# Moving operand copies, a row of maxima, a division and a projection by a few steps in an adaLN transformer block

## The chip, the core and the metric

The kernel runs on one core of one Trainium2 chip. The time is the device time of one execution in microseconds (us); of several runs the median is given. The core's engines work beside each other, each through its own instructions in order: TensorE (PE, matrix multiplication), VectorE (DVE), ScalarE (ACT), GpSimd (POOL), and SyncE (SP), which here issues nearly all DMA transfers. They wait for each other through semaphores.

## The reference

A transformer block on x of shape (4, 1024, 256), fp32, with conditioning vectors c that give shifts, scales and gates (sa, ca, ga, sb, cb, gb) per batch:

```python
h = _layernorm(x) * (1 + ca) + sa
x = x + ga * attention(h)            # 16 heads of 16 columns, softmax over 1024 keys
h = _layernorm(x) * (1 + cb) + sb
x = x + gb * ffn(h)
```

The attention is the usual one: `softmax(q k^T / 4) v`, then a projection. The second part, per 256 rows of x in the reference's shapes, is applied here per batch: 8 pairs of an encoder and a decoder reconstruct h (`relu(h W_enc + b) W_dec + b`); the one with the least mean squared error is chosen, and the chosen one's low-rank adapter (`relu(h W_down + b) W_up + b`) is added to a base product `h W_base + b`.

## The kernel before

**Tiles and steps.** Each batch has 16 heads, taken in 4 groups of 4 (`groups`, one entry per batch b and group g). Queries are split into two halves of 512, keys into 8 tiles of 128. One step handles one key tile for one group and one half of the queries, so a group takes `STEPS` = 16 steps and the whole run 256. In each step PE forms the transposed scores `pt` (L707; twice, for two pairs of heads), ACT takes their exponential into `es` (L715), and PE multiplies that with V into `pv` (L664, `weigh`), which also gathers the sum of exponentials. `pt` is a sum of two products: k times q, and a second matmul that subtracts the row maxima, held in the tile `mt` (two of them, for even and odd groups). A step cannot finish `pt` before its `mt` is there.

**Row maxima.** They are computed a group ahead, by `row_max` (L557): 32 pairs of scores `ps` for each group (L604), each reduced by DVE (L611), 16 pairs for each half of the queries. `wanted` (L1175) says how many pairs are to be done by a given step: a straight line between three points, the first one 19 pairs at step 0, the second 32 at step `NT - LEAD` = 3, the last 512 at step 243. When a half is complete, `to_row` (L562) turns the maxima into a row: PE transposes them (`pmx`, L564), DVE copies the result (`mfull`, L566), POOL splits it in two (`mrow`, L569 and L570), SP stores it to DRAM (`mdram`, L573) and brings it over into `mt` (L584). `defer(n, f)` calls f n steps later; outside the opening (`alone`), `store` comes one step after `to_row`, and `back` one step after that. They only fix places in SP's order: what SP waits for are semaphores.

**Operands.** Per batch and half of the columns, `qk_chunk` computes q and k in two parts and stores them to DRAM (L417, 1 MB each). `fetches` (L1185) brings the operands of each later group back by `expand` (L514): 8 copies of 256 KB on SP for each group (L525), due `n * STEPS + 1` for the n-th entry of `groups[2:]`, and only once the q and k they need are stored.

**Who decides the order.** PE's and SP's instructions are emitted in the order written out by the loop at L1281. It runs over pairs of steps and follows a pattern of letters: t for half a step's `pt`, S for scores of the row maxima, V for a step's `pv`, D for a tile of dense work, R for a decoder. Items of dense work lie in streams with conditions (`need`, `wait`, `at`); `to_row` is an item in the stream `urgent`, taken after the first V of a pair of steps. After step 16 the order on ACT, DVE and POOL is set by a scheduler.

**The end of a batch** (`post`, L721): projection of the attention result (`project`, L752), normalisation, encoders and decoders (L793, L814 to L822), `choose` (L833) with its gathers from DRAM, the two halves of `narrow` (L901: `pmid`, the chosen adapter's first product), and `final` (L958). It is spread over the next batch's steps. For the last batch part of it runs in the last steps and the rest after the loop (L1334 to L1348), where `all_of` takes a fixed number of items from one set of streams after another.

**Division.** The attention result is divided by its sums. In the last group the sums come straight from `ou` into `last_su`, and `scaled_last` (L646) does the reciprocal and the product on DVE, in two pieces of 256 columns: for the first half of the queries two steps after step 240, for the second after the loop.

Of the kernel before, what the change touches and what calls it, by code (L numbers as in the profile page):

```python
# [26 lines left out]
def tile_adaln_block(  # L27
# [22 lines left out]
    B, S, D = x.shape  # L50
    NE, _, FH = w_enc.shape
    R = w_down.shape[2]
    NT = S // P
    NC = D // P
    NG = D // (HG * HD)
    GC = P // (HG * HD)
    NPAIR = NE // 2
    SCALE = HD ** -0.5
    HALF = 512
# [220 lines left out]
    FULL = 0.86  # L280
# [4 lines left out]
    def defer(steps, f):  # L285
        later.append([steps, f])
# [8 lines left out]
    spare, alone, over = [0], [True], []  # L295
# [261 lines left out]
    def row_max(b, g):  # L557

        n = (b * NG + g) % 2
        mx = st.tile([P, NH, NH, HG, TH], F32, tag="mx", name=f"mx_{b}_{g}", bufs=2)  # L560

        def to_row(hq):  # L562
            pm = msc_tile([P, P], f"pmx_{b}_{g}_{hq}")
            nc.tensor.transpose(pm, mpad[n], ident)  # L564
            mfull = st.tile([HG * NT, P], F32, tag="mfull", name=f"mfull_{b}_{g}", bufs=1)
            nc.vector.tensor_copy(mfull, pm[: HG * NT, :])  # L566
            mrow = st.tile([HG * NT, 2, P], F32R, tag="mrow", name=f"mrow_{b}_{g}", bufs=1)
            eng = nc.vector if alone else nc.gpsimd
            eng.tensor_copy(mrow[:, 0, :], mfull)  # L569
            eng.tensor_tensor(mrow[:, 1, :], mfull, mrow[:, 0, :].bitcast(F32), ALU.subtract)  # L570

            def store():
                nc.sync.dma_start(  # L573
                    mdram[n][hq].rearrange("l r c -> r l c"),
                    mrow[hq * HG * TH : (hq + 1) * HG * TH].bitcast(F32),
                )
                if alone:
                    back()
                else:
                    defer(1, back)  # L580

            def back():
                for a in range(2):
                    nc.sync.dma_start(  # L584
                        mt[n][a * DUO : a * DUO + HG, hq * HALF : (hq + 1) * HALF].bitcast(F32),
                        mdram[n][hq, :, a * HG * TH // 2 : (a + 1) * HG * TH // 2, :].rearrange(
                            "l (i t) c -> l i (t c)", i=HG // 2
                        ),
                    )

            if alone:
                store()
            else:
                defer(1, store)

        for half in range(NH):
            pairs = [(i, half, t, h) for h in range(NH) for i in range(2) for t in range(TH)]
            for i, hq, t, h in pairs:
                q, k = duos["q", b, g, i], duos["k", b, g, i]
                t0 = hq * HALF + t * P  # L600
                ps = big_tile([P, 2, HALF], f"ps_{b}_{g}_{hq}_{t}_{h}_{i}")
                for a in range(2):
                    r = slice(a * DUO, (a + 1) * DUO)
                    nc.tensor.matmul(  # L604
                        ps[:, a, :],
                        q[r, t0 : t0 + P],
                        k[r, h * HALF : (h + 1) * HALF],
                        start=True,
                        stop=True,
                    )  # L610
                nc.vector.tensor_reduce(mx[:, h, hq, i::2, t], ps, AX.X, ALU.max, negate=True)  # L611
                if (i, hq, t, h) == pairs[-1]:
                    rows = mpad[n][:, : HG * NT].rearrange("p (q j t) -> p q j t", q=NH, t=TH)
                    nc.vector.tensor_tensor(rows[:, half], mx[:, 0, half], mx[:, 1, half], ALU.min)
                    defer(1, lambda half=half: urgent.append(("D", 0.0, [lambda: to_row(half)])))
                yield
# [26 lines left out]

    last_su = {}

    def scaled_last(h):  # L646
        su, part = last_su[h], aT_of[B - 1, h][:, NC - 1, :]
        for u in range(2):
            cols = slice(u * HALF // 2, (u + 1) * HALF // 2)
            nc.vector.reciprocal(su[:, cols], su[:, cols])  # L650
            nc.vector.tensor_tensor(part[:, cols], part[:, cols], su[:, cols], ALU.mult)

    def step_of(b, g):

        n = b * NG + g
        va = vaug[n % NV]
        ch, r0 = g // GC, (g % GC) * HG * HD
        acc = {}

        def weigh(h, kt, es):  # L660
            if kt == 0:
                acc[h] = accp.tile([P, HALF], F32, tag="acc", name=f"pv_{b}_{g}_{h}")
            for j in range(HG):
                nc.tensor.matmul(  # L664
                    acc[h][j * STRIP : (j + 1) * STRIP, :],
                    va[:, kt, j, :],
                    es[j // 2][:, j % 2, :],
                    start=(kt == 0),
                    stop=(kt == NT - 1),
                )  # L670
            if kt == NT - 1:
                if (b, h) not in aT_of:
                    aT_of[b, h] = wp.tile([P, NC, HALF], F32, tag="aT", name=f"aT_{b}_{h}", bufs=3)
                ou = wp.tile([P, HALF], F32, tag="ou", name=f"ou_{b}_{g}_{h}", bufs=1)
                nc.scalar.copy(ou, acc[h])
                to = slice(r0, r0 + HG * HD)
                at = aT_of[b, h][to, ch, :]
                if (b, ch) == (B - 1, NC - 1):
                    nc.sync.dma_start(at, ou[0::2, :])
                if (b, ch) == (B - 1, NC - 1):  # L680
                    if h not in last_su:
                        last_su[h] = wp.tile([P, HALF], F32, tag="su", name=f"su_{b}_{ch}_{h}", bufs=1)
                    nc.sync.dma_start(last_su[h][to, :], ou[1::2, :])
                    if g == NG - 1 and h < NH - 1:
                        defer(2, lambda: scaled_last(h))
                        defer(4, lambda: done.add((b, ch, h)))
                    return
                j0 = (g % GC) * HG

                def keep():  # L690
                    nc.sync.dma_start(at, ou[0::2, :])
                    nc.sync.dma_start(sdram[ch * NH + h][j0 : j0 + HG, :], ou[1::STRIP, :])
                    if g % GC == GC - 1:
                        defer(1, lambda: turned(b, ch, h))
                        defer(8, lambda: done.add((b, ch, h)))

                defer(1, keep)

        def begin(h, kt, i, es):

            pt = big_tile([P, 2, HALF], f"pt_{b}_{g}_{h}_{kt}_{i}")
            hs = slice(h * HALF, (h + 1) * HALF)
            q, k = duos["q", b, g, i], duos["k", b, g, i]
            for first in (True, False):
                for a in range(2):
                    r = slice(a * DUO, (a + 1) * DUO)
                    nc.tensor.matmul(  # L707
                        pt[:, a, :],
                        k[r, kt * P : (kt + 1) * P] if first else picks[i][r, :],
                        q[r, hs] if first else mt[n % 2][r, hs],  # L710
                        start=first,
                        stop=not first,
                    )
            e = wp.tile([P, 2, HALF], F32, tag="es", name=f"es_{b}_{g}_{h}_{kt}_{i}", bufs=4)
            nc.scalar.activation(e, pt, AF.Exp, scale=SCALE)  # L715
            es.append(e)

        return begin, weigh


    def post(b, last=False):  # L721
# [256 lines left out]
        recs.append(("done", (b, "r")))  # L978
        tail = [("need", (b, "r")), ("wait", 3), ("D", 0.1, [choose]), ("X", gate_out)]
        tail += [("X", lambda u=u: biased(u, "gbb")) for u in range(NT // 2)]  # L980
        tail += [("wait", 1), ("D", FULL, [lambda c=c: narrow(c) for c in range(NC)]), ("wait", 1)]
        each = [(u, t) for u in range(NT // 2) for t in range(2)]
        if last:
            first = [v for v in each if early(v[0])]
# [11 lines left out]
    STEPS = NH * NT  # L996
# [177 lines left out]

    def wanted(k):  # L1175

        ends = [(0, FIRST + 3), (NT - LEAD, PAIRS), (len(order) * NT - NT - LEAD, len(groups) * PAIRS)]
        for (k0, n0), (k1, n1) in zip(ends, ends[1:]):
            if k < k1:
                return n0 + (n1 - n0) * (k + 1 - k0) // (k1 - k0)  # L1180
        return ends[-1][1]
# [3 lines left out]
    def fetches():  # L1185

        moves = []
        for n, (b, g) in enumerate(groups[2:]):
            moves += [("at", n * STEPS + 1)] + [("need", (w, b, g // GC)) for w in "qk"]
            moves += [("X", lambda b=b, g=g, i=i: expand(b, g, i)) for i in range(2)]  # L1190
            if n + 2 >= NV:
                moves += [("need", ("v", b, NT // 2 - 1)), ("X", lambda b=b, g=g: fetch_v(b, g))]
        return moves
# [202 lines left out]
```

## Time and profile before

| what | us |
|---|---|
| median of 3 runs (lowest, highest) | 1140.43 (1139.66, 1143.99) |
| profiled execution, device time | 1141.97 |
| profiled execution, span of the program | 1140.1 |
| PE busy | 1079.2 |
| DVE busy | 797.2 |
| ACT busy | 702.6 |
| loop's last `pt` ends | 1070.4 |

The span is the time from the first to the last instruction of the program in the profiled execution. A group's row in the profile names the line, the engine, the operation, what it writes and reads, and the mean duration; in the timeline a bracket at the end of a row gives the idle time of that engine before it and what ended it. A wait is put down to the one that came last.

### The profile page before, as it was taken

The numbers are of one execution on the slowest core, as the hardware profiler recorded it, in microseconds if no ns is written. First come the engines' busy times: TensorE is split into PE (matmuls) and PEld (weight loads), VectorE is DVE, ScalarE is ACT, GpSimd is POOL, SyncE is SP. The second block draws the span as 40 slices with busy tenths as digits, with TensorE's granted clock in tenths as the row PEclk, the third lists the DMA queues.
The fourth block names the chain that finished last, engine by engine and source line by source line (L and its number), as shares of the span: only waits on it lengthen the run. The fifth ranks groups of instructions, "written<-read, shape, count | busy, mean of one in ns | idle before, by whom it ended". The sixth has DMA issues, their size and how long they took to land. (4 is left out here: it accounts for less than half of the span.)

```text
span 1140.1 us, 16544 instructions
## 1 busy us (share of the span) xinstructions
PE 1079.2 (95%) x6371; PEld 482.7 (42%) x6371; DVE 797.2 (70%) x958; ACT 702.6 (62%) x953; POOL 262.3 (23%) x309
## 2 busy tenths in 40 slices
PE   8989899999999999999999999999998999999995
PEld 3433334443444444444544443333544334334433
DVE  5687677667767676777678777877688777872373
ACT  3246566666556677776455777776465677754672
POOL 2214234213243121112435100003221000041103
PEclk9899999999999999999999999999999999999997
DMA  6522423232340302123150303021140200002001
GB/s 185 103 66 90 153 78 119 85 118 71 130 153 39 126 16 91 53 78 100 53 183 6 128 7 99 16 83 27 57 142 2 90 8 16 20 23 85 20 0 49
DMA packets 57799, 84.63 MB, mean 74 GB/s; under 512 B 24940, under 2 KB 40324, under 8 KB 55928
## 3 DMA queue, kind: packets, MB, share of 16 engines
q1 hardware_dynamic: 55824, 80.16, 21.9%
q0 software_dynamic: 1088, 2.36, 0.8%
q8 instruction: 50, 0.82, 0.3%
q10 hardware_dynamic: 808, 1.05, 0.3%
q14 instruction: 29, 0.24, 0.1%
HBM read 52.15 MB, written 24.06 MB: 67 GB/s over the span
## 5 line engine op out<-in xcount | busy, mean ns | idle before, releaser
L611 DVE TENSOR_REDUCE mx<-ps 128x2 f32<-128x1024 f32 x512 | 614.5, 1221 | 196.8 <-PE ps L604 191.2
L715 ACT ACTIVATE es<-pt 128x1024 f32<-128x1024 f32 x512 | 509.4, 1021 | 250.0 <-PE pt L707 229.4
L664 PE MATMUL pv<-es,vaug 128*32 128x512 f32 x2048 | 274.8, 607 | 0.5
L604 PE MATMUL ps<-k,q 64*128 64x512 f32 x1024 | 238.9, 458 | 15.9 <-DVE mx L611 11.6
L707 PE MATMUL pt<-q,k 64*128 64x512 f32 x1024 | 231.1, 435 | 11.1 <-DVE mx L611 7.7
L707 PE MATMUL pt<-mt,pick 64*128 64x512 f32 x1024 | 209.9, 393 | 3.7 <-DMA mt<-mdram 3.7
L604 PEld LDWEIGHTS ps<-k,q 64*128 64x128 f32 x1024 | 97.7, 184 | 223.2 <-issue 91.8
L707 PEld LDWEIGHTS pt<-q,k 64*128 64x128 f32 x1024 | 99.9, 185 | 116.0 <-DVE mx L611 87.7
L822 ACT ACTIVATE df<-df,fbias 128x512 f32<-128x512 f32 x128 | 91.1, 713 | 56.2 <-DVE df L817 56.2
L707 PEld LDWEIGHTS pt<-mt,pick 64*128 64x128 f32 x1024 | 100.6, 186 | 16.4 <-DMA mt<-mdram 4.0
L817 DVE TENSOR_TENSOR df<-pr,h2T 128x1024 f32<-128x1024 f32 x64 | 77.4, 1223 | 21.4 <-PE pr L814 14.9
L664 PEld LDWEIGHTS pv<-es,vaug 128*32 128x32 f32 x2048 | 40.6, 108 | 102.0 <-issue 90.4
L569 POOL CAST mrow<-mfull 32x128 fp32r<-32x128 f32 x31 | 8.7, 281 | 278.6 <-DVE mfull L566 270.7
L814 PE MATMUL pr<-he,wdec 64*128 64x512 f32 x256 | 64.6, 601 | 3.3 <-ACT es L715 3.2
L793 PE MATMUL ph<-h2T,wenc 128*128 128x512 f32 x128 | 62.4, 615 | 0.5 <-ACT h2T L350 0.4
L928 PE MATMUL pf<-wbg,h2T 128*128 128x256 f32 x128 | 37.6, 426 | 1.9 <-DVE x L948 1.9
L319 POOL TENSOR_TENSOR rstd_n<-ve_n,neghalf 128x4 f32<-128x4 f32 x16 | 16.5, 1031 | 86.3 <-DVE ve_n L317 83.5
L505 POOL COPY vaug<-vi 128x512 f32<-128x512 f32 x13 | 8.5, 657 | 111.1 <-DMA vi<-vdram 85.7
L793 PEld LDWEIGHTS ph<-h2T,wenc 128*128 128x128 f32 x128 | 22.0, 189 | 28.4 <-issue 25.2
L466 PE MATMUL pvp<-wqkv,hT 128*128 128x256 f32 x128 | 33.0, 404 | 0.0
L814 PEld LDWEIGHTS pr<-he,wdec 64*128 64x128 f32 x256 | 23.1, 185 | 22.3 <-ACT es L715 6.3
L801 ACT ACTIVATE he<-ph,fbias 128x512 f32<-128x512 f32 x32 | 22.0, 686 | 16.7 <-PE ph L793 16.7
(150 smaller groups left out, 786.0 us busy)
## 6 DMA issues: line engine op xcount, KB each, us to landing
q<-qdram SPq DMA_DIRECT2D x56, 256.0 KB
k<-kdram SPq DMA_DIRECT2D x56, 256.0 KB
qdram<-qhl SPq DMA_DIRECT2D x7, 1024.0 KB
kdram<-khl SPq DMA_DIRECT2D x7, 1024.0 KB
xin<-in_L_attn_x_dram SPq DMA_DIRECT2D x16, 256.0 KB
vdram<-vo SPq DMA_DIRECT2D x16, 256.0 KB
aT<-ou SPq DMA_DIRECT2D x32, 128.0 KB
x<-in_L_attn_x_dram SPq DMA_DIRECT2D x8, 512.0 KB
```

Source lines behind the costliest of these rows:

```text
L466: nc.tensor.matmul(pv[:, t, :], hT[:, c, t0 : t0 + P], wqkv[:, c, 2 * D : 3 * D], start=(c == 0), stop=(c == NC - 1),)
L604: nc.tensor.matmul(ps[:, a, :], q[r, t0 : t0 + P], k[r, h * HALF : (h + 1) * HALF], start=True, stop=True,)
L611: nc.vector.tensor_reduce(mx[:, h, hq, i::2, t], ps, AX.X, ALU.max, negate=True)
L664: nc.tensor.matmul(acc[h][j * STRIP : (j + 1) * STRIP, :], va[:, kt, j, :], es[j // 2][:, j % 2, :], start=(kt == 0), stop=(kt == NT - 1),)
L707: nc.tensor.matmul(pt[:, a, :], k[r, kt * P : (kt + 1) * P] if first else picks[i][r, :], q[r, hs] if first else mt[n % 2][r, hs], start=f ...
L715: nc.scalar.activation(e, pt, AF.Exp, scale=SCALE)
L793: nc.tensor.matmul(s["ph"], wenc[:, c, 2 * pr : 2 * pr + 2, :].rearrange("p n h -> p (n h)"), s["h2T"][:, c, hs], start=(c == 0), stop=(c ...
L801: nc.scalar.activation(s["he", pr, h], s["ph"], AF.Relu, bias=benc_of(pr))
L814: nc.tensor.matmul(two[:, i, :], wdec[r, pr, c * P : (c + 1) * P], he[r, :], start=True, stop=True)
L817: nc.vector.tensor_tensor(df, two, h2T[:, c, hs].unsqueeze(1).to_broadcast([P, 2, HALF]), ALU.subtract)
L822: nc.scalar.activation(df[:, i, :], df[:, i, :], AF.Square, bias=bdec_of(e, c), accum_out=s["acc"][:, e, c, h : h + 1],)
L928: nc.tensor.matmul(po[u][:, t, :], s["h2T"][:, c, t0 : t0 + P], s["wbg"][:, c, :], start=(c == 0), stop=False,)
```

## The change

There are five edits. In `row_max`, the row of the second half of group 0 (`soon`) is stored and brought over at the place where it is made, without the two deferrals; all other rows are as before, the first half's included. In `scaled_last`, the division of the last group is done in four pieces of 128 columns; for the first half of the queries the pieces stand in steps 242, 243, 244 and 245, and the half counts as done at step 246, not 244. For batches 0 to 2, `narrow` waits two steps after `choose` and the additions, not one. In `wanted`, the second point lies at step 5, not 3, so that the line that follows starts two steps later and ends where it did. In `fetches`, the operands of the first later group (n = 0) are due at step 15, not 1; for all others `max` gives the old step.

```diff
+        soon = b + g == 0
...
-                if alone:
+                if soon:
                     back()
                 else:
                     defer(1, back)
...
-            if alone:
+            if soon:
                 store()
             else:
                 defer(1, store)
...
-    def scaled_last(h):
+    def scaled_last(h, us=range(4)):
         su, part = last_su[h], aT_of[B - 1, h][:, NC - 1, :]
-        for u in range(2):
-            cols = slice(u * HALF // 2, (u + 1) * HALF // 2)
+        for u in us:
+            cols = slice(u * HALF // 4, (u + 1) * HALF // 4)
             nc.vector.reciprocal(su[:, cols], su[:, cols])
             nc.vector.tensor_tensor(part[:, cols], part[:, cols], su[:, cols], ALU.mult)
...
-                        defer(2, lambda: scaled_last(h))
-                        defer(4, lambda: done.add((b, ch, h)))
+                        for u in range(4):
+                            defer(2 + u, lambda u=u: scaled_last(h, [u]))
+                        defer(6, lambda: done.add((b, ch, h)))
...
-        tail += [("wait", 1), ("D", FULL, [lambda c=c: narrow(c) for c in range(NC)]), ("wait", 1)]
+        tail += [("wait", 1 if last else 2), ("D", FULL, [lambda c=c: narrow(c) for c in range(NC)]), ("wait", 1)]
...
-        ends = [(0, FIRST + 3), (NT - LEAD, PAIRS), (len(order) * NT - NT - LEAD, len(groups) * PAIRS)]
+        ends = [(0, FIRST + 3), (NT - LEAD + 2, PAIRS), (len(order) * NT - NT - LEAD, len(groups) * PAIRS)]
...
-            moves += [("at", n * STEPS + 1)] + [("need", (w, b, g // GC)) for w in "qk"]
+            moves += [("at", max(n * STEPS + 1, STEPS - 1))] + [("need", (w, b, g // GC)) for w in "qk"]
```

## The prediction

> **What bounds the kernel now.** I read the page's busy rows first, then what TensorE (PE) waits for, then the timeline around each place that the diff names.
>
> ```profile
> PE 1079.2 (95%) x6371; PEld 482.7 (42%) x6371; DVE 797.2 (70%) x958; ACT 702.6 (62%) x953; POOL 262.3 (23%) x309
> PEclk9899999999999999999999999999999999999997
> ```
>
> PE is busy 95% of 1140.1 us, and executes in order, so what is to be gained or lost is its idle time: 54 us over the span. About 4 us of it lies in the first steps (57 to 85 us, waits for VectorE, DVE), 8.9 in the tail after the loop (from 1073), the rest is scattered. The view of PE's waits has these among its rows:
>
> ```profile
> PE ps L604 <- DVE mx L611: 11.6, 26, 1.5
> PE pt L707 <- DVE mx L611: 7.7, 11, 1.2
> PE pt L707 <- DMA mt<-mdram: 3.7, 1, 3.7
> PE pf L928 <- DVE x L948: 1.9, 1, 1.9
> ```
>
> Total, number, longest. Two single stalls stand out. The first (3.66 us, step 16) is the row of maxima `mt` landing late; the second (1.91 us at 1028 us) is PE waiting for DVE while `scaled_last(0)` divides. The timeline of step 16 names the culprit:
>
> ```profile
> 118.84 0.32 SPq L573 DMA_DIRECT2D mdram<-mrow  x1
> 119.26 1.16 SPq L525 DMA_DIRECT2D q<-qdram  x2
> 120.47 1.22 SPq L525 DMA_DIRECT2D k<-kdram  x2
> 121.74 1.23 SPq L525 DMA_DIRECT2D q<-qdram  x2
> 123.01 1.24 SPq L525 DMA_DIRECT2D k<-kdram  x2
> 124.30 1.31 SPq L584 DMA_DIRECT2D mt<-mdram  x2
> 128.59 0.97 PE L707 MATMUL pt<-mt,pick 64*128 64x512 f32 x2 [3.66 <-DMA mt<-mdram]
> ```
>
> Eight operand copies (L525) stand in SP's queue between the row's store (L573) and its way back (L584). All other 31 rows come in time, most with 5 to 10 us to spare.
>
> **The chain that the change leans on.** An undisturbed row, from PE's transpose to the way back:
>
> ```profile
> 145.49 0.33 PE L564 MATMUL pmx<-ident,mpad 128*128 128x128 f32 x1
> 145.92 0.28 DVE L566 COPY mfull<-pmx 32x128 f32<-32x128 f32 x1 [0.65 <-PE pmx L564]
> 146.27 0.28 POOL L569 CAST mrow<-mfull 32x128 fp32r<-32x128 f32 x1 [23.84 <-DVE mfull L566]
> 146.63 0.45 POOL L570 TENSOR_TENSOR mrow<-mfull,mrow 32x128 fp32r<-32x128 f32 x1
> 147.11 0.33 SPq L573 DMA_DIRECT2D mdram<-mrow  x1
> 148.56 1.38 SPq L584 DMA_DIRECT2D mt<-mdram  x2
> ```
>
> Store 1.62 us after the transpose, way back 3.07 to 4.45, its last packet 5.49 (the trace's DMA packets); at step 16 PE resumed 0.4 after the last packet. So a clean row needs **5.9 us** from `pmx` to its first use. Now its first use is about 12 us after `pmx` (145.5 to 157.6).
>
> **Part 1, the pace (`NT - LEAD + 2`).** The built order of both programs shows what a shift of 2 in one table entry does: `to_row` moves two steps later for every row from step 8 to step 120 (15 rows; from step 128 on the rounding to pairs of steps gives the old places). `pmx` then stands in the pair of steps just before its use. What PE has left between them is 3 `ps` pairs, 5 `pt` pairs, one `pv` set, and whatever tile of dense work falls there. The old trace prices this as the time from the end of the `pv` two steps later to the use: 5.2 us with a tile (152.4 to 157.6, and five more alike), 3.2 with none (242.9 to 246.2), 6.1 with a tile and a pair. The slack of two steps is spent, and the chain is longer than most of the rooms. Row by row, with what the new order puts in the way:
> - steps 8, 40, 56, 72, 88: clean, 5.9 - 5.2 = 0.7 each, 3.5 in all.
> - step 24: an `rstd` (1.03) stands between the two `mrow` operations on POOL: 1.7.
> - steps 32, 64, 80: a 1 MB store of `khl` or `qhl` now stands between the row's store and way back. The old row of step 88 had that and landed at 6.18 instead of 5.49, so 6.6 - 5.2 = 1.4; at 80 POOL is a little late as well, 1.7. Together 4.5.
> - step 48: such a store and no tile: 6.6 - 3.25 = 3.35.
> - steps 96, 104: room 6.1, nothing. Step 112: 0.5. Step 120: 0.4.
> - step 16: below.
>
> That is 13.95 us. Nothing covers it, as PE waits in order with all later work behind it.
>
> **Part 2, operands from step 15.** The copies of group 2 were issued at step 13, when their sources were ready, and now at step 15. But the row of step 16 has moved by the same two steps, and the built order of SP is the old one: store, eight copies, way back. Store at 1.6, way back 5.46 later, issue 1.31, and 2.98 to the use as at 125.61 to 128.59: 11.35 against a bare room of 3.25. The stall of 3.66 becomes **8.1**, so +4.4. The copies themselves are wanted at step 21 and are not late. The other groups' dates do not change (`max` binds for n = 0 alone).
>
> **Part 3, `soon`.** The row of step 8 is now issued without the two deferrals. SP has nothing else between, and waits on semaphores rather than steps; worth 0 here. If that cover went, it would be a step, some 4 us.
>
> **What the slower start returns.** DVE had 13 reductions of 1.2 us to do in three steps, and now has five steps. Of the 4.06 us that PE idles from 57 to 85 us I take back 2.5 (bounds 0 and 4).
>
> **Part 4, division in pieces.** Two reciprocals of 256 columns take 1.75 us each; four of 128 should take about half each, plus a small overhead. At most it saves the 1.91 stall and the slow clock after it (1.7), and at least nothing, since DVE's sum of work in steps 241 to 245 is unchanged and its own reductions for `ps` are late next: I take -2.5. One rule speaks against counting on more. The multiply of L651 took 0.36 to 0.41 us three times and 1.53 once, while POOL was adding `gbb` to `x`. The Trainium skill (SBUF — State Buffer, its rules on the shared port pair) says that a DVE operation with two SBUF inputs and a GpSimd operation that reads SBUF lock each other out for the whole instruction. By the row, four pieces cost four times 0.2; by the rule, each piece may wait for a POOL addition (1.25 us), 4 us more. The additions are 5 us long in all and the pieces are now spread over four steps, so one or two meet them.
>
> **Part 5, narrowing two steps behind.** All four `pmid` (541.7, 790.8, 1014.8, 1125.2) start without idle time on PE: nothing to gain. It delays batch 2's output, hence the load of `x` for batch 3 (step 247 to 249) and the first projection (251 to 253; `done` at +6 alone would allow it). The second projection then is the last tile of the loop, and its normalisation, hidden beside steps 254 and 255 until now, is exposed: from the end of `ppj` (1067.14) to the first transpose is 4.6 us, of which 2.7 lie beside the last `pv`: 1.9. Then `ppj_3_2` comes after one `ph` instead of four, and the last division (5.3 us after `pv` for the DMA, then 2.0 for two pieces) makes it wait 2 us. The decodes begin about 10 us later but with three `he` already out, and ACT, which sets the end (14 squares, each with a read of its sum, in 9.99 us without a break), catches most of that up. I count **+2.8** (0 to 5).
>
> **The clock.** Each half-speed stretch in the clock record is 3.41 us and costs 1.7. In the loop there are three, after stalls of 3.66, 1.21 and 1.91 us; stalls of 1.53, 1.20, 1.20 and 1.16 had none. The Trainium skill (TensorE: Matmul & The Clock Gate, What's actually happening) says that the clock halves after at least one idle window of about 3.4 us. By the rule only step 16's stall would pay, as it does now: +0. By the rows, step 48's 3.35 pays 1.7, and of the four of 1.4 to 1.7 about one: I take **+3** and keep 0 and 10 as bounds.
>
> **Sum.** 13.95 + 4.4 - 2.5 - 2.5 + 2.8 + 3 = +19.2 us. Stalls also let DVE catch up, so some of the 19.3 us of `mx` waits vanish: about -1. The profiled execution took 1141.97 (span 1140.1), 1.5 above the median of 1140.43; on the median the sum gives **1158.5**.
>
> **Rivals.**
> - *Only the bare rows stall.* If the chain is nearer to 5 us than 5.9, steps 16 and 48 alone pay: 4.4 + 2.7 + 2 - 5 + 2.8 = +7, 1147. For it: the 0.7 of five rows is small beside what I can measure of a landing. Against it: every clean row in the trace agrees within 0.2.
> - *The clock falls at each stall.* Then 11 stalls cost 1.7 each: 1174. For it: 1.21 us was enough once. Against it: four like it were not.
> - *Faster.* One mechanism: the evener pace frees DVE early, and the row still arrives before step 16's use because SP gets to it ahead of the copies. Then 3.66 and 1.7 of clock go, with 2.5 early and 2.5 at the division, less 2.8: -7.6, 1133. It decides if `pmx` to landing is under 3.2 us at step 16. The built order speaks against it.
> - *Nothing moves* (0.5%, 5.7 us, is about what a measurement of this kernel can tell from no change): the stalls are half of what I count and the gains whole, 1141.
>
> **Chances.** Forecast 0.66, bare rows 0.13, clock 0.12, nothing 0.05, faster 0.04. Slower therefore 0.91. The range takes in the bounds: without clock and tail and with stalls 0.4 shorter it is +8, with the clock's upper part and the tail's +30.
>
> **What would show it.** Waits of PE for `mt<-mdram` go from 1 to about 13, from 3.7 us to some 22; the longest is at step 16, near 8 us; rows from step 128 on wait for nothing. Idle time from 57 to 85 us falls to about 1.5. The `pf` wait for `x` shrinks, and PE waits before the first `ptn_n` after the loop. I am wrong if rows at steps 24 to 88 arrive without a wait: then the 5.9 or the 5.2 is wrong.

## The result, and the profile after

| | before | after |
|---|---|---|
| median of 4 runs each, us | 1141.60 (1139.66 to 1143.99) | 1182.83 (1178.01 to 1183.53) |
| ratio, 95% interval | | 1.0351 (1.0316 to 1.0386) |
| profiled execution: span, us | 1140.1 | 1181.0 |
| mean granted TensorE clock in it | 0.984 | 0.968 |

The change makes the kernel slower by some 41 us. The direction and the main mechanism were forecast; 1158.5 was too low, and so was the upper end of the range (+30 us).

First the page of the changed kernel, busy rows and clock:

```profile
PE 1098.8 (93%) x6371; PEld 492.1 (42%) x6371; DVE 798.9 (68%) x966; ACT 703.7 (60%) x953; POOL 262.3 (22%) x309
PEclk8899899999899999999999999999999999999898
```

Read the PE row against the one of before: the same 6371 instructions are busy for 1098.8 us instead of 1079.2. That is 19.6 us more for the same work. The rest of the span, 82.2 us instead of 60.9, is idle: 21.3 us more. So **the loss, as it is booked, has two halves of about equal size**: TensorE waits longer, and it is slower when it works. The clock records say the same in another way: half of all half-speed time in the span is 38.0 us after and 17.7 before, some 20 us more. Booked is not yet caused: the runs with fillers, below, show how much comes back when the slow stretches go.

Where the waits are, by the view of PE's waits (total, number, longest, in us):

```profile
PE pt L711 <- DMA mt<-mdram: 17.7, 12, 7.5
PE pt L711 <- DVE mx L614: 14.8, 12, 5.4
...
PE ptn_n L347 <- DVE xh_n L324: 2.9, 2, 2.7
```

The first row is the late row of maxima: 3.7 before, so +14.0. The second was 7.7: +7.1, of which 5.4 is one single wait that the prediction has nothing of. The third was 1.7: the exposed normalisation in the tail. The row of `pf` waiting for `x` (1.9) is gone from the list.

Where the slow work is, by the view of stretches, for the same stretch of work in both programs (from the use of step 16's row to that of step 64's; bounds, length, then busy time and instructions of PE, PEld, DVE, ACT, POOL, then clock, DMA share, GB/s). Before, then after:

```profile
128.00:306.00 178.00, 170.99 (x1076) 75.22 (x1076) 125.55 (x142) 112.18 (x124) 50.07 (x57) 0.99 0.31 103
```
```profile
134.00:330.00 196.00, 179.81 (x1078) 78.47 (x1078) 125.07 (x142) 112.66 (x125) 49.97 (x57) 0.95 0.27 93
```

DVE, ACT and POOL do the same work in the same time. PE's same matmuls take 8.8 us more, at a clock of 0.95 instead of 0.99, and it idles 9.2 us more. These 48 steps alone bring 18 us.

The longest wait, at step 16, in the timeline of the changed kernel:

```profile
123.39 0.33 PE L567 MATMUL pmx<-ident,mpad 128*128 128x128 f32 x1
...
125.02 0.32 SPq L576 DMA_DIRECT2D mdram<-mrow  x1
125.43 1.16 SPq L525 DMA_DIRECT2D q<-qdram  x2
126.64 1.22 SPq L525 DMA_DIRECT2D k<-kdram  x2
127.91 1.23 SPq L525 DMA_DIRECT2D q<-qdram  x2
129.20 1.23 SPq L525 DMA_DIRECT2D k<-kdram  x2
130.47 1.31 SPq L587 DMA_DIRECT2D mt<-mdram  x2
...
134.58 0.97 PE L711 MATMUL pt<-mt,pick 64*128 64x512 f32 x2 [7.48 <-DMA mt<-mdram]
```

From `pmx` to the use it is 11.19 us (11.35 was reckoned). The last line also shows the clock: two matmuls take 0.97 us, where the same pair took 0.39 to 0.40 a few us earlier.

And a wait that I had not foreseen, at step 61, in the same kernel's timeline:

```profile
298.82 4.85 POOL L324 TENSOR_SCALAR xh_n<-xin,mv_n,rstd_n 128x256 f32<-128x256 f32 x4
...
303.61 0.62 POOL L443 CAST qhl<-fu_q 128x512 fp32r<-128x512 f32 x1
...
305.63 0.34 SPq L417 DMA_DIRECT2D qdram<-qhl  x1
...
306.08 0.38 SPq L632 DMA_DIRECT2D rdram<-rs  x1
...
309.71 0.64 SPq L636 DMA_DIRECT2D su<-rdram  x1
...
310.40 0.45 SPq L94 DMA_DIRECT2D xin<-in_L_attn_x_dram  x1
...
314.02 0.43 DVE L312 BATCH_NORM_STATS2 bs_n<-xin 128x6 f32<-128x256 f32 x1 [6.78 <-DMA xin<-in_L_attn_x_dram]
...
315.63 0.80 PE L711 MATMUL pt<-q,k 64*128 64x512 f32 x2 [5.39 <-DVE mx L614]
```

Read it from the end. PE waits for a reduction; DVE has it queued behind `bn_stats`, which waits 6.78 us for `xin`; SP issues `xin` only at 310.40, since `su<-rdram` ahead of it waits for the store of 306.08 to land, and that store stood behind the `qdram` store, which waited for `qhl`; POOL made `qhl` after a normalisation of 4.85 us. That normalisation is late because its two loads stand on SP behind the way back of step 56's row. They stood there before as well; what has moved is the row, and the loads with it. Before, then after:

```profile
266.30 1.35 SPq L584 DMA_DIRECT2D mt<-mdram  x2
267.70 0.90 SPq L94 DMA_DIRECT2D xin<-in_L_attn_x_dram  x2
```
```profile
289.17 1.34 SPq L587 DMA_DIRECT2D mt<-mdram  x2
290.56 0.90 SPq L94 DMA_DIRECT2D xin<-in_L_attn_x_dram  x2
```

Step 56's first use of its row is at 275.88 before and at 291.63 after, so the loads leave 1.1 us ahead of it instead of 8.2.

### The profile page after: what moved, and what is told of

It is laid out like the page before. It is cut to its first block, busy times and chain, and to the rows that moved or that the text cites. A ratio compares the mean times of both kernels' runs of the same rounds, so it can differ in the third digit from the quotient of the medians.

```text
span 1181.0 us, 16557 instructions
## 1 busy us (share of the span) xinstructions
PE 1098.8 (93%) x6371; PEld 492.1 (42%) x6371; DVE 798.9 (68%) x966; ACT 703.7 (60%) x953; POOL 262.3 (22%) x309
## 5 line engine op out<-in xcount | busy, mean ns | idle before, releaser
L667 PE MATMUL pv<-es,vaug 128*32 128x512 f32 x2048 | 279.3, 618 | 0.3 <-ACT ou L678 0.2
L607 PE MATMUL ps<-k,q 64*128 64x512 f32 x1024 | 242.9, 461 | 14.4 <-DVE mx L614 10.3
L711 PE MATMUL pt<-q,k 64*128 64x512 f32 x1024 | 235.1, 439 | 20.8 <-DVE mx L614 14.8
L711 PE MATMUL pt<-mt,pick 64*128 64x512 f32 x1024 | 219.5, 399 | 18.0 <-DMA mt<-mdram 17.7
L711 PEld LDWEIGHTS pt<-q,k 64*128 64x128 f32 x1024 | 103.0, 187 | 126.4 <-DVE mx L614 94.8
L711 PEld LDWEIGHTS pt<-mt,pick 64*128 64x128 f32 x1024 | 105.9, 189 | 36.0 <-DMA mt<-mdram 23.3
L797 PE MATMUL ph<-h2T,wenc 128*128 128x512 f32 x128 | 64.9, 632 | 0.4 <-ACT h2T L350 0.4
L952 DVE TENSOR_TENSOR x<-pf,x 128x512 f32<-128x512 f32 x16 | 10.8, 687 | 37.1 <-PE pt L711 25.1
L645 POOL TENSOR_TENSOR aT<-aT,su 128x512 f32<-128x512 f32 x14 | 17.9, 1280 | 78.3 <-DMA su<-rdram 76.8
L805 ACT ACTIVATE he<-ph,fbias 128x512 f32<-128x512 f32 x32 | 22.0, 686 | 21.3 <-PE ph L797 21.3
```

The source lines that it names most:

```text
L607: nc.tensor.matmul(ps[:, a, :], q[r, t0 : t0 + P], k[r, h * HALF : (h + 1) * HALF], start=True, stop=True,)
L667: nc.tensor.matmul(acc[h][j * STRIP : (j + 1) * STRIP, :], va[:, kt, j, :], es[j // 2][:, j % 2, :], start=(kt == 0), stop=(kt == NT - 1),)
L711: nc.tensor.matmul(pt[:, a, :], k[r, kt * P : (kt + 1) * P] if first else picks[i][r, :], q[r, hs] if first else mt[n % 2][r, hs], start=f ...
L797: nc.tensor.matmul(s["ph"], wenc[:, c, 2 * pr : 2 * pr + 2, :].rearrange("p n h -> p (n h)"), s["h2T"][:, c, hs], start=(c == 0), stop=(c ...
L805: nc.scalar.activation(s["he", pr, h], s["ph"], AF.Relu, bias=benc_of(pr))
```

## The experiments

Each run has its own runs of the kernel before beside it (medians 1140.64 to 1142.68); ratios are to those.

**One part at a time.** First the pace put back in the changed kernel:

```diff
-        ends = [(0, FIRST + 3), (NT - LEAD + 2, PAIRS), ...
+        ends = [(0, FIRST + 3), (NT - LEAD, PAIRS), ...
```

> The changed kernel with the table entry of the pace put back (NT - LEAD), all other edits kept. Theory (the pace makes nearly all of the loss, by stalls on the row of maxima and the half-speed stretches after them): the rows come in time again, waits of PE for mt<-mdram under 1 us in all, because the copies of step 15 now stand behind the way back of step 16's row; the half-speed stretches of the first 370 us go but for one or none; about 1141 us, between 1135 and 1147. Rival (the order of narrowing and the tail make a good part of it): 1155 or more. Rival (the copies at step 15 are late by themselves): a stall on q or k at step 16 to 24 shows.

1138.95 us, ratio 0.9982 (0.9971 to 0.9993). The row of waits for `mt` is gone altogether, and between 65 and 1066 us there is no half-speed stretch. **Without the pace there is no loss**; the other four edits together are a small gain.

The pace alone, the same edit the other way round in the kernel before:

> The kernel before with the pace edit alone (NT - LEAD + 2). Theory: nearly the whole loss, 1172 to 1183 us; some 14 us of waits for mt, longest about 7 us at step 16, twelve or so half-speed stretches. Rival (the loss needs the other edits, or the tail): under 1165 us.

1166.24 us, ratio 1.0219 (1.0185 to 1.0253): between the two readings. The pace alone costs 25.6 us, not 41; in the company of the other edits it costs some 42 to 44 (43.9 between the medians, 42.2 by the ratios). Step 16 shows a part of the reason, in the timeline of the pace-only kernel:

```profile
118.03 1.24 SPq L525 DMA_DIRECT2D k<-kdram  x2
...
125.43 0.32 SPq L573 DMA_DIRECT2D mdram<-mrow  x1
126.87 1.72 SPq L584 DMA_DIRECT2D mt<-mdram  x2
...
128.96 0.56 PE L707 MATMUL pt<-mt,pick 64*128 64x512 f32 x1 [1.45 <-DMA mt<-mdram]
```

The copies of step 13 are done with on SP before the row, now two steps later, gets there: 1.45 us of wait (and 0.70 for the row's second half) instead of 3.66 before and 7.48 in the whole change.

The copies at step 15 alone (`max(n * STEPS + 1, STEPS - 1)`, nothing else):

> The kernel before with the operand copies at step 15 alone. Theory: the row of step 16 comes before the copies on SP, so the stall of 3.66 us and its half-speed stretch (1.7) go: 1135 us, 1133 to 1138. Rival (something else is late there next): 1140 to 1142, no difference.

1135.51 us, ratio 0.9947 (0.9933 to 0.9962), as expected: the stall of step 16 and the half speed after it are gone. So either edit takes the copies out from between the row's store and its way back, and **both together put them there again**. The direct test, the changed kernel with the copies at step 13 again:

> The changed kernel with the operand copies of group 2 back at step 13. Theory (with the pace shifted, copies issued at step 13 are ahead of the row on SP; it is step 15 that puts them back between its store and its way back): the wait for mt at step 16 falls from 7.48 to about 1.5 us as in the pace-only kernel, -6 us and some clock: 1173 to 1177. The prediction on record took the eight copies to stand there because of the pace. Rival (the copies stand between either way): 1181 to 1184.

1175.06 us, ratio 1.0299 (1.0284 to 1.0313), 7.8 us less than with the copies at step 15; the wait at step 16 is 1.51 us.

The pace shifted by one step instead of two:

> The changed kernel with the pace shifted by 1 instead of 2. Theory (a threshold: the row has 5.9 us to go and gets about 12 us without the shift): with one pair of steps fewer moved, only the rows that the rounding moves are late; if the rounding to pairs moves the same rows, the time is that of the changed kernel, 1175 to 1185; if it moves none, about 1141. Rival (a gradual cost in proportion to the shift): about 1160.

1145.73 us, ratio 1.0042 (1.0031 to 1.0053). No row moved (each `pmx` to use is as without the shift, 10 to 18 us) and none is waited for: the rows' cost does not grow with the shift, it comes all at once when the rounding to pairs of steps moves the rows. The 7 us over the kernel with no shift lie in steps 240 to 248 of the profile (+9.4): a wait of 3.06 us among the pieces of the division, and 13.65 us of half speed from there on.

The division in pieces alone, then the narrowing alone:

> The kernel before with the last division in four pieces alone (done two steps later, as in the change). Prediction's term: -2.5 us (0 to -4), 1138. Theory now: the stall of 1.91 at 1028 us goes, but another DVE wait takes its place (the changed kernel has 2.77 us before a pt in the same steps), so about nothing: 1139 to 1142. Rival: done being two steps later pushes a projection behind the loop: 1143 or more.

> The kernel before with narrowing two steps behind the choice alone. Prediction's term: 0 in the loop and +2.8 (0 to 5) in the tail together with the division. Theory now: +3.5 us, 1142 to 1146, seen in the steps 192 to 200 and in the tail after the loop. Rival: the tail's part comes from the division's done at +6 alone, then 1140 to 1141 here.

Pieces: 1139.13 us, ratio 0.9984 (0.9972 to 0.9996), tail unchanged (69.7 us from the end of the last `pt`, as before). Narrowing: 1144.80 us, ratio 1.0033 (1.0021 to 1.0046), its tail 74.2 us. So 4.5 of the tail's +5.3 us in the changed kernel (75.0) are the narrowing's, and the division's later `done` shows no part in it; tails of programs with the same edits there differ by up to 1.5 us. The wait that the prediction named first for the tail is in the narrowing-only kernel's waits as well:

```profile
PE ptn_n L347 <- DVE xh_n L324: 2.9, 2, 2.7
```

The stall of 1.91 us at 1028, which the pieces were to remove, is 0.7 us in the pace-only, 0.6 in the copies-only and absent in the narrowing-only profile, where the division is as before. So it is no fixed cost of the division in two pieces; the multiply ahead of it took 1.53 us in that profile and 0.82 in the copies-only one. The kernel before has one profile, so how often it stalls there is open.

**Pace and pieces together.** The profiles of all runs, those below included, settle where the wait among the pieces comes from. With the pace, by one step or by two, seven pairs of scores fall in steps 240 to 248, without it six. In all eleven profiles that have both the pace and the pieces, TensorE waits 2.6 to 3.1 us there for a reduction, and these steps take 39.6 to 45.7 us. In those with the pieces and no pace they take 36.0 to 36.4, with the pace and the old division 37.1, and no reduction is waited for longer than 1.2 us. Neither edit does it alone.

**The deferrals.** Every row's store and way back issued as soon as the row is there:

```diff
-        soon = b + g == 0
+        soon = True
```

> The changed kernel with every row's store and way back issued as soon as the row is there, not only the first group's. Theory (between store and way back the row is bound by its own transfers, not by the steps, except where something else has been put between): the copies of step 15 now stand behind step 16's row, so the wait of 7.48 us falls to about 1.5, and the rows of steps 32, 64 and 80 lose the 1 MB store between, 0.5 to 1 us each; the others stay: 1172 to 1177. Rival (the deferral costs every row): the waits at 24, 40, 48 and 72 go as well, under 1168.

1169.70 us, ratio 1.0247 (1.0214 to 1.0281): more gain than my theory gave, less than the rival. In its waits:

```profile
PE pt L711 <- DMA mt<-mdram: 8.8, 11, 2.1
```

Half of the 17.7 us is gone, 5.8 of it at step 16, which falls to 1.68. The rows of 64 and 80 need 5.5 us to their use instead of 6.2 and 6.6 and make PE wait 0.2 us at most. Of the four waits that the rival named, that of step 24 goes; those of 40, 48 and 72 stay (1.0, 1.7 and 2.3 us). The second half of the way back was issued half a us sooner (at 4.35 instead of 4.82 us after `pmx`). Bound by its transfers alone, a row needs 5.3 to 5.5 us, not the 5.9 of the prediction.

**The clock.** PE was kept at work in four of its waits by repeating a matmul that needs no `mt` (its result is overwritten):

```diff
+            fill = {2: 13, 4: 4, 6: 4, 9: 3}.get(2 * n + h, 0) if kt + i == 0 else 0
-            for first in (True, False):
+            for x, first in enumerate([True] * fill + [True, False]):
...
-                        stop=not first,
+                        stop=x < fill or not first,
```

> The changed kernel with TensorE kept busy in four of its waits for mt: ahead of the first use of the rows of steps 16, 32, 48 and 72 the matmul of the same tile that needs no mt is repeated (26, 8, 8 and 6 extra matmuls, some 6.0, 1.8, 1.8 and 1.4 us; each repeat overwrites the one before). Theory (half the loss is the clock, which falls in the window after one with a long idle part): the row comes at the same time, idle time falls by about 11 us and is filled with useless work, and the half-speed stretches at 129, 200, 262 and 368 us go: -6 us, 1174 to 1179. Rival (the clock is no cost of these stalls): 1182 to 1185.

1183.60 us, ratio 1.0365 (1.0322 to 1.0407): inconclusive, as 28 matmuls took 3.48 us, half of what was reckoned, and 5.25, 1.42, 1.60 and 2.82 us of the four waits stayed idle. With `{2: 28, 4: 8, 6: 9, 9: 7}`:

> The changed kernel with longer fillers than the run before (56, 16, 18 and 14 repeats; a repeat took 0.12 us there, half of what was reckoned, so that 5.3, 1.4, 1.6 and 2.8 us of the waits stayed idle). Theory (the clock is judged by windows of 3.41 us and falls after one that is idle for more than half): the waits for mt at the four rows shrink under 0.8 us with the row no earlier, three or four half-speed stretches go, -5 us: 1175 to 1180. Rival (the fall isn't from these stalls): the stretches stay, 1182 to 1185.

1178.74 us, ratio 1.0327 (1.0313 to 1.0342), the page and the waits:

```profile
PEclk9999999999899999999999999999999999999898
```
```profile
PE pt L712 <- DMA mt<-mdram: 5.8, 10, 1.2
```

The rows come no earlier (step 16's use is 11.29 us after `pmx`, 11.19 without filler), but from 57 to 305 us there is no half-speed stretch, where the changed kernel has 20.5 us of it between 67 and 265 us. From the use of step 8's row to that of step 56's it takes 3.3 us less (188.56 instead of 191.86): PE did useless work instead of waiting, and what changed besides is the speed of the useful work. The gain is smaller than what is booked: in the changed kernel 17.1 us of that stretch are at half speed, 5.8 of them idle, so that the slow work costs 5.7, and 3.3 come back. A part of the rest turns into waits for reductions (4.2 us instead of 2.8). In the whole, the intervals of the two programs still touch (the wait at step 61 was 6.79 us in this profile instead of 5.39), so the stretch shows the gain and the median only agrees with it.

**The wait at step 61.** All loads of `x` on ACT's queue, then only batch 3's:

```diff
-        nc.sync.dma_start(xt, src[...])
+        (nc.scalar if b else nc.sync).dma_start(xt, src[...])
```

> The changed kernel with the loads of x for batches 1 to 3 issued from ACT's queue instead of SP's. Theory (at step 56 the later way back of the row stands on SP ahead of the two x loads, the normalisation slips behind, POOL's qhl after it, the qdram store and the next x load after that, until DVE waits 6.8 us with reductions behind it): the stall of 5.4 us before pt at step 61 and its half-speed stretch of 6.83 go, -7 us, 1172 to 1178. Rival (the stall comes from the order of DVE or from the late q itself): it stays, 1181 to 1184.

> The changed kernel with only batch 3's loads of x (steps 56 to 64) issued from ACT's queue. Theory (the row's way back holds up these loads on SP, and the normalisation, qhl and the next load after it): steps 56 to 64 lose their 8.6 us as in the run that moved all batches' loads, without that run's new waits at step 8 to 16: 1172 to 1177. Rival (the stretch got shorter there only because the earlier stalls had shifted everything): 1181 to 1184.

1190.91 us, ratio 1.0449 (1.0406 to 1.0493), and 1184.35, ratio 1.0359 (1.0333 to 1.0384): both miss. Steps 56 to 64 did get 8.6 and 8.5 us shorter and their wait vanished, but on ACT the issue of a load waits for its buffer with the exponentials behind it: ACT stood still for 5.00 us in the first run and 8.60 in the second, and PE waited 3.42 and 6.08 us for an exponential. In the first run PE also waited 8.97 and 7.50 us for the two halves of step 16's row, whose way back took SP 8.97 us to issue; why is not shown. The first loads allowed two steps earlier on SP (`3 * STEPS + 6` for `3 * STEPS + 8`), then also with the copies at step 13:

> The changed kernel with batch 3's first loads of x allowed two steps earlier (step 54 instead of 56), so that on SP they stand ahead of the store and the way back of the row that the pace moved to steps 54 to 56. Theory: xin lands in time, DVE's wait of 6.8 us and TensorE's of 5.4 at step 61 go with the half-speed stretch, steps 56 to 64 lose 8 us, nothing else changes: 1172 to 1177. Rival (the su copy on SP, which waits for its store, delays the next load anyway): the wait shrinks by less than half, 1179 to 1184.

> As the run before, and the operand copies of group 2 back at step 13. Theory (the two collisions on SP are independent): the gains add, -7 and -8 from the changed kernel, 1165 to 1169; what then is left over the kernel without the pace edit, about 28 us, is the row waits, their clock, and the waits that the profile shows beside them. Rival (one hides the other): 1172 or more.

1187.98 us, ratio 1.0396 (1.0342 to 1.045), and 1182.47, ratio 1.0363 (1.0320 to 1.0407). My theory of that edit fell. POOL in the first of them:

```profile
286.18 3.63 POOL L324 TENSOR_SCALAR xh_n<-xin,mv_n,rstd_n 128x256 f32<-128x256 f32 x3
289.76 0.28 POOL L572 CAST mrow<-mfull 32x128 fp32r<-32x128 f32 x1
290.04 1.21 POOL L324 TENSOR_SCALAR xh_n<-xin,mv_n,rstd_n 128x256 f32<-128x256 f32 x1
```

The normalisation that came in time now stood in front of the row, whose way back was late by 4.84 us, and 3.02 us of the wait at step 61 were left. What was left had another cause on SP, which the last run takes alone: the copy `su<-rdram` of that step issued by GpSimd.

```diff
-            nc.sync.dma_start(su, ...)
+            (nc.gpsimd if (b, ch, h) == (0, 1, 0) else nc.sync).dma_start(su, ...)
```

> The changed kernel with one transfer moved from SP's queue to GpSimd's: the copy su<-rdram of batch 0 at step 61, which GpSimd itself uses next. Theory (x of step 62 waits on SP behind su, and su for its own store): x is issued right behind rdram<-rs, some 3 us sooner, DVE's wait of 6.8 us falls to 3 to 4, TensorE's wait at step 61 from 5.4 to about 2, 2 to 4 us of it and of the clock go: 1178 to 1181. Rival (x is late for another reason): TensorE's wait stays over 4.5 us, 1182 to 1185.

1177.19 us, ratio 1.0322 (1.0285 to 1.0358), a little better than expected; 3.3 us of the gain lie in steps 56 to 64 of the profile. In its timeline:

```profile
299.27 0.38 SPq L632 DMA_DIRECT2D rdram<-rs  x1
299.69 0.91 SPq L94 DMA_DIRECT2D xin<-in_L_attn_x_dram  x1
...
303.89 0.75 DVE L312 BATCH_NORM_STATS2 bs_n<-xin 128x6 f32<-128x256 f32 x2 [3.44 <-DMA xin<-in_L_attn_x_dram]
```

`xin` leaves 0.42 us after the `rdram` store instead of 4.32; DVE waits 3.44 instead of 6.78, PE 2.60 instead of 5.39. **A transfer that waits on SP holds up every transfer behind it**, here an unrelated load.

**The best of it.** Copies at step 15 and the division in pieces, without the other three edits:

> The kernel before with two of the change's edits alone: the copies at step 15 and the division in pieces. Theory (each showed its own gain, at step 16 and at steps 240 to 248, far from each other): 1133 us, 1131 to 1136, ratio about 0.993. Rival (they meet, as pace and copies do): no better than the copies alone, 1135.5.

1134.76 us, ratio 0.9949 (0.9932 to 0.9965): faster than both kernels, but no better than the copies alone, so the pieces add nothing that can be measured.

## Why the prediction was right and wrong

- *Where the sum was short.* 18.2 us forecast, 40.9 between the profiled executions. Slow work was put at 3 and measured 19.6: 16.6 short. Idle time was put at 15.2 (18.2 less 3) and measured 21.3: 6.1 short.
- *Bound and chain.* Right: PE in order, a row two steps later, stalls at steps 8 to 88, none from 128 on. Sum of the stalls 22.05 forecast (13.95 and 8.1), 17.7 measured. Row by row it is less exact: 24 gave 0.62 for 1.7, 56 nothing for 0.7, 88 at most 0.2 for 0.7, but 32 gave 2.34 for 1.4 and 72 1.79 for 0.7. The chain of 5.9 us was 0.5 too long for a clean row and too short where the second half of the way back came late.
- *Step 16.* 8.1 forecast, 7.48 measured. The reason given, that the built order of the whole change keeps the eight copies between, was right; the two edits apart behave otherwise, which the single runs show.
- *Part 3, `soon`.* Worth 0 at step 8 was not tested alone; the pace-only kernel, which lacks it, needs 6.18 us from `pmx` to that row's use, the changed kernel 5.82. For the other rows a deferral does cost, not by the steps themselves but by what SP issues in between: without it 8.9 us of waits go, 5.8 of them at step 16.
- *Part 1's other queues.* **This is the first step that failed.** I asked what the new order puts in the way of the row, at every row, but not what the row is in the way of. At step 56 two loads of `x` stand behind it on SP and are moved with it, 7.1 us nearer to the row's use; the 5.39 us at step 61 follow, with 6.83 us of half speed.
- *The clock, +3 (0 to 10).* **This is the step that carried the miss.** The same matmuls took 19.6 us more. By the records, half speed in the loop (60 to 1105 us) lasts 40.9 us instead of 10.2, of which at most half, 15 us, is lost; the rest lies in the opening and the tail. I took a stall as the unit and asked whether it was long enough. The unit that fits, worked out in the last section, is the idle time in a fixed window of 3.41 us: the windows ahead of the three stretches in the profile before hold 3.41, 1.42 and 1.82 us of it. The rival in which the clock falls at each stall (1174) was nearer, but it left out the stall at step 61.
- *Part 4, -2.5.* The pieces alone gave 2.0 us, and nothing beside the copies. In the whole change they make a wait of their own, longer than the old one, since the pace puts one more reduction among them. Three pieces run together on DVE:

```profile
1060.16 1.75 DVE L653 RECIPROCAL su<-su 128x128 f32<-128x128 f32 x2
1061.83 1.95 DVE L654 TENSOR_TENSOR aT<-aT,su 128x128 f32<-128x128 f32 x2
1063.70 0.94 DVE L653 RECIPROCAL su<-su 128x128 f32<-128x128 f32 x1
1064.57 1.16 DVE L614 TENSOR_REDUCE mx<-ps 128x2 f32<-128x1024 f32 x1
```

  PE waited 2.77 us for the first of the reductions behind the last reciprocal. Deferring the pieces by a step each does not space them on DVE. The lock-out that the prediction weighed is in these rows: the two multiplies of the second row took 0.68 and 1.35 us, each ending 0.15 us after an addition of POOL (1.3 us long), where the undisturbed pieces of the second half took 0.23 to 0.28. That is 1.5 us more on DVE.
- *Part 5, +2.8 in the tail.* 5.3 measured, 4.5 of it with the narrowing alone; the exposed normalisation costs 2.7 where 1.9 was reckoned, and the division, to which I gave a part, shows none.
- *The slower start, -2.5.* PE's idle time from 57 to 85 us fell from 4.06 to 3.47 us: 0.6.

The parts add up to 35 us of the 41: 25.6 for the pace, 3.7 for narrowing, -2.0 for pieces, 7.8 for the copies meeting the pace. The pace meeting the pieces brings 3.3 more in steps 240 to 248 of the profile (39.6 us instead of 36.3 without the pace). The last 3 us stay open; they are no more than single executions of the changed kernel lie apart (1178.0 to 1183.5).

## What to carry to other kernels

When a step is moved in an order that is fixed by hand, go through each in-order queue that it issues on and read both ways: what now stands before it, and what stands behind it and is moved with it. Two edits that each clear a queue can collide when made together, so build their combined order rather than add their gains. And price TensorE's idle time twice, once as waiting and once as the half-speed work that follows, of which a part may hide in waits that are there anyway.

## What the runs showed of the hardware

The clock is not judged by the stall. In the clock records of all 18 profiles the half-speed stretches begin on a grid of 3.413 us (the phase differs from execution to execution, and within one it holds to 3 ns). I cut PE's time on that grid, without the first 20 windows and up to the last matmul, and took each window at full speed with the idle time in it:

| idle in the window, us | windows | next one at half speed |
|---|---|---|
| 1.8 or more | 73 | 72 |
| 1.6 to 1.8 | 8 | 6 |
| 1.4 to 1.6 | 42 | 22 |
| 1.2 to 1.4 | 41 | 10 |
| under 1.2 | 5374 | 0 |

So somewhat over half a window of idle time is enough, several short waits in one window count together (at 330 us in the changed kernel 1.25 us in pieces of at most 0.71 did it), and a wait of 1.2 to 3 us may or may not pay according to where the grid falls. That fits how far executions of one program lie apart: in 49 runs of the kernel before the fastest took 1136.8 us at a mean granted clock of 0.989, the slowest 1145.8 at 0.979. The Trainium skill (TensorE: Matmul & The Clock Gate, What's actually happening) has the free-running window of 3413 ns but asks for a whole idle window; here somewhat over half of one did it in 72 of 73 cases, and the measurement decides. The way back to full speed is less regular. All 43 windows at half speed with 1.2 us or more of idle time were followed by another at half speed, but so were 27 of the 139 with less, up to three in a row over work almost without a gap (13.65 us in the runs with the pace by one step, all `x` on ACT's queue, and the short filler); no run explains that.
